# A four-layer graph network on one core: TensorE signals once per two units of nodes in layer 0 and once per quad in layer 3

## The chip, the cores and the metric

The kernel runs on one core of one Trainium2 chip. The metric is the device time of one execution in microseconds (us). The engines are TensorE (PE, with its weight loads shown apart as PEld), VectorE (DVE), ScalarE (ACT), GpSimd (POOL) and SyncE (SP), which only starts transfers here. Each engine works through its own queue of instructions in order. An engine that needs another's result waits on a semaphore, which the other one raises when a marked instruction is complete.

## The reference, cut to what matters

There are 8192 nodes with 32 features, and 262144 edges sorted by destination. Four layers run one after the other, each followed by a residual sum and a layer normalisation.

```python
x = ln(x + segment_sum(einsum('ei,eio->eo', x[src], weight[edge_type]), dst))   # layer 0, 64 types
x = ln(x + segment_sum(x[src] * edge_weight[:, None], dst))                     # layer 1
x = ln(x + segment_sum(x[src], dst))                                            # layer 2
h = relu(edge_feat @ W1 + b1)                                                   # layer 3
w = (h @ W2 + b2).reshape(e, 4, 8, 8)
m = products of s[src], v[src], edge_sh with w      # 8 scalars, 8 vectors of 3
x = ln(x + segment_sum(m, dst) + self_part(x))
```

## The kernel before

The change lies in `raw_layers`, in layers 0 and 3. A small class `Flow` holds an engine's queue: `mark(ins)` lets an instruction raise the engine's semaphore by one and returns the value that then stands for "done", and `after(mark)` makes the engine wait for such a value. A wait on a mark therefore covers all that the marking engine did before it.

**Gathers.** In both layers POOL fetches rows for 128 edges at a time, one indirect transfer each (`indirect`, L387), 2048 per layer. Layer 0 fetches rows of `fytab` (node features already multiplied with each type's weight), layer 3 rows of `fxtab`. POOL runs ahead of the other engines, but waits for a PE mark before it goes on: in layer 0 the rows of group g + 12 wait for marks of group g (L665, L671; the constant `AHEAD` is 12), in layer 3 those of quad q + 8 wait for the mark of quad q (`fetch_rows`, L842, called at L926; `AHEAD` is 8). Inside `gathers` it also waits for the transfers of two batches before, eight transfers to a batch.

**Layer 0** walks over 256 groups of 1024 edges. For group g, DVE makes a one-hot of the destinations (`one_hot`, L509), waits for the rows, and splits them into three bf16 parts (`parts`, L624 to L629). PE adds the parts up by destination (eight matmuls, L662) into a slot of bank 0 or 1 of the accumulator memory: four groups share a bank, and the two banks take turns. After four groups, `bank_out` (L635) reduces the bank to `win` with one DVE instruction. Every 32 groups `windows` (L499) and `normalize` (from L458) finish a chunk of 1024 nodes.

In the same loop, from group 8 on, `matrices` makes the dense matrices that layers 1 and 2 will use: 256 sets, nearly one per group, finished with group 251. For a set, DVE writes three one-hots (L562, L564, L567); PE turns them into four units of eight nodes (L576), each unit filling two of the banks 2 to 6 with 16 matmuls; PE marks each unit, and ACT copies its banks out in four instructions (L581, L582). SP then stores the set to `famat` and `fcmat` (L586, L587). `oh_free`, `bank_free` and `agg_free` hold the marks that allow a one-hot, a bank or an accumulator to be written again.

**Layers 1 and 2** load the stored matrices and multiply them (L761, L764). They begin when all of layer 0 is done.

**Layer 3** walks over 512 quads of 512 edges; two quads make one of the 256 groups, and eight quads a batch of edge data. One pass q of the loop issues on PE, in this order:

- H (`hidden(q + 2)`, L899, even q only): the first matrix of the edge network for two quads, then a mark on which ACT applies the relu (L907);
- w (L923): the second matrix for quad q into one of two pairs of banks, then a mark, on which DVE's products of quad q wait (L960, L963, L967);
- a (L932): the sums by destination of the older quad c = q - `LAG3`, with `LAG3` = 4, into bank 0 or 1 by the parity of its group, then a mark.

The waits of these: w(q) needs the relu of quad q and DVE's products of quad q - 2 to be done (the pair of banks is read). a(c) needs DVE's pass c + 2 and, for the first quad of a group, that DVE has read out the group two before (`agg_free`).

DVE's pass q does, in order: `factors` for the next two quads (L863 to L870, even q, waits for the gathered rows), small parts of quads q - 2 and q - 1 (L946, L951), the one-hot (L509), the products of quad q, and, when quad q - `LAG3` - 1 ends a group, the read-out of that group (L988, L989, L991), which waits for the mark of its a. `p` has six buffers; the one of quad q is free when a(q - 6) is marked. Every 32 groups `windows` and `normalize` finish a chunk here too.

Of the kernel before, what the change touches and what calls it, by code (L numbers as in the profile page):

```python
# [15 lines left out]
AF = mybir.ActivationFunctionType  # L16
OP = mybir.AluOpType
AX = mybir.AxisListType
# [3 lines left out]
P = 128  # L22
N = 8192
E = 262144
D = 32
R = 64
NB = N // P
# [7 lines left out]
GT = 8  # L35
GG = TT // GT
WS = N // GG
WT = 32
LC = 8
# [106 lines left out]
def raw_layers(tc, x, a, w0, w1, b1, w2, si, m, bad):  # L146
# [34 lines left out]
    def now(f):  # L181
        return (f.sem, f.n)
# [211 lines left out]
    n = 0  # L394
# [88 lines left out]
    def windows(c, acc, free):  # L483

        d0 = c * LC
        todo = []
        for j in [0, 1, 2, 3, -2, -1, 4]:
            lo, hi = 0, LC
            while 4 * (d0 + lo) + j < 0:
                lo += 1  # L490
            while 4 * (d0 + hi - 1) + j >= GG:
                hi -= 1
            if lo < hi:
                todo.append((j, lo, hi))
        wv = win.rearrange("p (d j) f -> p d j f", j=4)
        PE.after(*free)
        for n, (j, lo, hi) in enumerate(todo):
            g0 = 4 * (d0 + lo) + j
            ins = PE.e.matmul(acc[:, lo * D:hi * D].rearrange("p (d f) -> p d f", f=D),  # L499
                              shift[:, P - WS * j:2 * P - WS * j], wv[:, g0 // 4:g0 // 4 + hi - lo, g0 % 4, :],  # L500
                              start=(n == 0), stop=(n == len(todo) - 1))
        return PE.mark(ins)

    def ready(c):

        return min(GG, 4 * (LC * (c + 1) - 1) + 5)

    def one_hot(o, t, n):
        return V.e.tensor_tensor(o, iota[:, None, :].to_broadcast([P, n, P]),  # L509
                                 rel[:, t:t + n, None].to_broadcast([P, n, P]), op=OP.is_equal)  # L510
# [34 lines left out]

    acc_free = [None]
    oh_used = [None, None]
    bank_free = {k: (acc_free[0] if k == 2 else None) for k in range(2, 7)}
    st_ld = [Landing(tc, f"st_m{k}") for k in range(2)]
    w_up = [None]  # L550
    units = [0]

    def matrices(i):

        b, pp, k0 = i % 2, i // 2, 16 * (i % 2)
        WB = 8
        if i % WB == 0:
            n = min(WB * 16, CB * 16 - i * 16)
            V.after(now(V))
            own(V, V.e.tensor_copy(w_ps[:, 0:n], meta_w.rearrange("p n k -> p (n k)")[:, i * 16:i * 16 + n]))  # L560
        V.after(oh_used[b])
        own(V, V.e.tensor_tensor(oh_k[:, b, :, 0, :], iota[:, None, 0:64].to_broadcast([P, 16, 64]),  # L562
                                 meta_k[:, pp, k0:k0 + 16, None].to_broadcast([P, 16, 64]), op=OP.is_equal))
        V.e.tensor_tensor(oh_l[:, b], iota[:, None, :].to_broadcast([P, 16, P]),  # L564
                          meta_l[:, pp, k0:k0 + 16, None].to_broadcast([P, 16, P]), op=OP.is_equal)
        wo = (i % WB) * 16
        vm = V.mark(V.e.tensor_tensor(oh_k[:, b, :, 1, :], oh_k[:, b, :, 0, :],  # L567
                                      w_ps[:, wo:wo + 16, None].to_broadcast([P, 16, 64]), op=OP.mult))
        PE.after(vm)
        for q in range(4):  # L570
            bk = [2 + (2 * units[0] + h) % 5 for h in range(2)]
            PE.after(*(bank_free[b5] for b5 in bk))
            for j in range(4):
                for h in range(2):
                    hs_ = slice(64 * h, 64 * h + 64)
                    ins = PE.e.matmul(bank[:, bk[h], :].rearrange("p (c s j) -> p c s j", s=64, j=4)[:, :, :, j],  # L576
                                      oh_l[hs_, b, 4 * q + j, :], oh_k[hs_, b, 4 * q + j], start=True, stop=True)
            pm = PE.mark(ins)
            A.after(pm, st_ld[b].mark() if q == 0 and st_ld[b].n else None)
            for h in range(2):  # L580
                A.e.activation(st_c[:, b, q, h], bank[:, bk[h], 0:256], AF.Copy)  # L581
                bank_free[bk[h]] = am = A.mark(A.e.activation(st_a[:, b, q, h], bank[:, bk[h], 256:512], AF.Copy))  # L582
            units[0] += 1
        oh_used[b] = pm
        S.after(am)
        st_ld[b].add(S.e.dma_start(amat[:, 2048 * i:2048 * (i + 1)], st_a[:, b].rearrange("p u h c -> p (u h c)")))  # L586
        st_ld[b].add(S.e.dma_start(cmat[:, 2048 * i:2048 * (i + 1)], st_c[:, b].rearrange("p u h c -> p (u h c)")))  # L587


    NS = TT // WT  # L590
    NO = 4
    oh_free = [None] * NO
    agg_free = [freed[0], freed[0]]
    G.after(r0, *y_done)
    V.after(*y_done)
    PE.after(*freed)
    FIRST = 8
    made = 0
    done = 0
    per = 4  # L600
    AHEAD = 12
    landed = {}
    sums_of = {}
# [25 lines left out]
        prev_parts[0] = V.mark(V.e.tensor_tensor(part[2], tf(r), tf(x_ps), op=OP.subtract))  # L629
        return prev_parts[0]  # L630

    def bank_out(n):

        V.after(sums_of[per * n + per - 1])
        agg_free[n % 2] = vm = V.mark(V.e.tensor_reduce(  # L635
            win[:, per * n:per * (n + 1), :], bank[:, n % 2, 0:per * 3 * D].rearrange("p (g c f) -> p g f c", c=3, f=D),
            AX.X, OP.add))
        return vm

    prev_parts = [None]  # L640
    for g in range(AHEAD):
        for h in range(2):
            fetch_rows(g, h, None)
    for g in range(GG + 2):
        if g >= 2 and (g - 2) % per == per - 1:
            vm = bank_out((g - 2) // per)
            while done < NB // LC and ready(done) <= g - 1:
                acc = bank[:, (g - 2) // per % 2, 0:LC * D]
                agg_free[(g - 2) // per % 2] = vm = normalize(0, done, acc, windows(done, acc, (vm,)), x_a, x_b)
                done += 1  # L650
        if g >= GG:
            continue
        h, bk, c = g % NO, (g // per) % 2, g % per
        if g == FIRST // 2:
            V.after(slots(), x_in)
        V.after(oh_free[h])
        one_hot(oh[:, h], g * GT, GT)
        PE.after(parts(g))
        if c == 0:
            PE.after(agg_free[bk])  # L660
        for t in range(GT):
            ins = PE.e.matmul(bank[:, bk, 3 * c * D:3 * (c + 1) * D], oh[:, h, t, :],  # L662
                              xp[:, g % 4, t].rearrange("p c f -> p (c f)"), start=(t == 0), stop=(t == GT - 1))
        oh_free[h] = sums_of[g] = PE.mark(ins)
        fetch_rows(g + AHEAD, 0, sums_of[g])  # L665
        if g >= FIRST:
            upto = min(CB, (g - FIRST + 1) * CB // (GG - FIRST - 4))
            while made < upto:
                matrices(made)
                made += 1  # L670
        fetch_rows(g + AHEAD, 1, now(PE))  # L671
    stored = [ld.mark() for ld in st_ld]


# [124 lines left out]
    vm = cut(2, WT, 3, 8)  # L799
    MW = 344  # L800
    NP, NO = 6, 6
    LAG3 = 4
    p = cut(NP, 4, MW)
    pr = cut(2, 4, 64)
    red = cut(2, 4, 8)
# [86 lines left out]
    def hidden(q):  # L892

        s = q // 8
        k = s % 3
        PE.after(batch[s]["e"], quad.get(q - 1, {}).get("h", h_free))
        for h in range(2):
            r = q % 4 + h
            ins = PE.e.matmul(bank[64 * h:64 * h + 64, 2, :], w1_s[r * D:(r + 1) * D, :],  # L899
                              ef[r * D:(r + 1) * D, k, (q % 8) // 4, :], start=True, stop=True,  # L900
                              tile_position=(r * D, 64 * h))
        pm = PE.mark(ins)
        if q % 8 == 6:
            ef_free[k] = pm
        for h in range(2):
            A.after(pm, quad.get(q + h - 4, {}).get("w"))
            quad[q + h] = dict(h=A.mark(A.e.activation(hs[0:64, (q + h) % 4], bank[64 * h:64 * h + 64, 2, :], AF.Relu,  # L907
                                                       bias=b1_s[64 * h:64 * h + 64])))
# [2 lines left out]
        fetch_rows(q)  # L911
    factors(0)
    PE.after(c_in, *zf)
    hidden(0)
    for q in range(NQ + LAG3 + 2):

        if q % 2 == 0 and q + 2 < NQ:
            hidden(q + 2)
        if q < NQ:
            k, wp = w_bank()  # L920
            PE.after(quad[q]["h"], w_free[k])
            for t in range(4):
                ins = PE.e.matmul(wp[:, t, :], hs[0:65, q % 4, t * P:(t + 1) * P], w2_s[0:65], start=True, stop=True)  # L923
            quad[q]["w"] = PE.mark(ins)
            quad[q]["k"] = k, wp
            fetch_rows(q + AHEAD)  # L926
        c = q - LAG3
        if 0 <= c < NQ:
            g = c // 2
            PE.after(quad[c + 2]["v"], agg_free[g % 2] if c % 2 == 0 else None)  # L930
            for t in range(4):
                ins = PE.e.matmul(bank[:, g % 2, 0:MW], oh[:, c % NO, t, :], p[:, c % NP, t, :],  # L932
                                  start=(c % 2 == 0 and t == 0), stop=(c % 2 == 1 and t == 3))
            quad[c]["a"] = PE.mark(ins)

        prev = (V.sem, V.n)
        if q % 2 == 0 and q + 2 < NQ:
# [533 lines left out]
```

## Time and profile before

| What | Value |
|---|---|
| median of 5 runs | 6433.94 us (6429.66 to 6434.11) |
| the profiled execution: its own time | 6430.87 us |
| the profiled execution: its span | 6429.0 us |
| PE / PEld / DVE busy | 4776.1 / 3448.2 / 4364.1 us |
| ACT / POOL busy | 1755.0 / 3972.4 us |
| first gather of layer 0, last gather of layer 0 (start) | 225.3, 2805.3 us |
| first gather of layer 3, last gather of layer 3 (start) | 3812.9, 6383.2 us |

The profile takes one execution and shows when each engine worked. The share of busy time is an average over four layers with different limits, so the stages are read one by one. For a group of instructions the profile gives the count, the busy time, the mean length of one, and the idle time of the engine just before them with what ended that idle time. "issue" there is the time in which the engine waited for nothing that the profile shows. In the timeline each row has the start, the length, the engine and the line; several instructions in a row are merged, and the brackets hold the idle time before the row. Matmul ends are modelled and overlap the next matmul.

### The profile page before, as it was taken

The page shows a single profiled execution, that of the slowest core. Times are in us where ns is not written, and L with a number is a line of the kernel's source. Part 1 is how long each engine was busy: PE and PEld are TensorE (multiplying, and loading weights), DVE is VectorE, ACT ScalarE, POOL GpSimd, SP SyncE. Part 2 cuts the span into 40 slices and gives each one's busy share as a digit, 9 for nine tenths or more (in the row PEclk, how much of TensorE's full clock was granted, in tenths as well). Part 3 has the DMA queues.
Part 4 walks back from the last instruction along what each step waited for, and adds up shares of the span by engine and source line. Part 5 has one row for each costly group of instructions (what it writes and reads, how often), then busy time and mean ns, then how long its engine had stood idle before and what let it go on. Part 6 is the DMA issues. An engine that isn't in the chain of part 4 may idle for free.

```text
span 6429.0 us, 89476 instructions
## 1 busy us (share of the span) xinstructions
PE 4776.1 (74%) x34036; PEld 3448.2 (54%) x34036; DVE 4364.1 (68%) x9246; ACT 1755.0 (27%) x4886; POOL 3972.4 (62%) x4174
## 2 busy tenths in 40 slices
PE   7356666566666565644446879999999999999998
PEld 3145555565556555532223446666666666666665
DVE  4288878888888888830000028788888888888887
ACT  5345444454445454520000001111111111111111
POOL 2677777777777777730000027777777777777775
PEclk7578878887778888777777979999999999999999
DMA  9457766666666666779999961111111111111111
GB/s 349 162 138 183 181 178 173 181 181 181 172 180 183 178 185 167 190 263 431 432 431 412 398 240 28 28 28 29 28 28 29 28 28 28 29 28 29 28 29 21
DMA packets 290756, 999.51 MB, mean 155 GB/s; under 512 B 99021, under 2 KB 175886, under 8 KB 250638
## 3 DMA queue, kind: packets, MB, share of 16 engines
q1 hardware_dynamic: 155742, 916.89, 38.0%
q0 software_dynamic: 134144, 73.67, 11.6%
q8 instruction: 272, 4.46, 0.3%
q10 hardware_dynamic: 432, 3.15, 0.2%
q14 instruction: 166, 1.36, 0.1%
HBM read 521.39 MB, written 471.99 MB: 155 GB/s over the span
## 4 chain that ended last, share of the span: by engine, by line
DMA 27%; PE 24%; POOL 20%; DVE 19%; issue 8%; ACT 1%; POOLq 0%; SPq 0%; DVEq 0%; ACTq 0%
POOL f_arena L387 20%; DMA f_arena<-fytab,f_row 8%; PE bank L932 8%; DMA f_arena<-famat 8%; PE bank L923 6%; DMA f_arena<-fxtab,f_src 6%; DVE f_arena L564 4%; DMA f_arena<-fcmat 3%; PE bank L761 2%; PE bank L576 2%; DVE f_arena L562 2%; DVE f_arena L567 2%; PE bank L764 2%; DVE f_arena L509 2%; DMA fytab<-f_arena 1%
## 5 line engine op out<-in xcount | busy, mean ns | idle before, releaser
L387 POOL DMA_INDIRECT f_arena<-fxtab,f_src x2048 | 1947.4, 951 | 1630.5 <-PE bank L730 1006.7
L387 POOL DMA_INDIRECT f_arena<-fytab,f_row x2048 | 1957.0, 956 | 652.5 <-issue 555.3
L576 PE MATMUL bank<-f_arena 64*128 64x128 f32 x16384 | 1356.3, 333 | 757.0 <-DVE f_arena L567 751.3
L576 PEld LDWEIGHTS bank<-f_arena 64*128 64x128 f32 x16384 | 1280.7, 242 | 823.1 <-DVE f_arena L567 789.3
L932 PE MATMUL bank<-f_arena 128*128 128x344 f32 x4096 | 1306.7, 461 | 0.0
L581 ACT ACTIVATE f_arena<-bank 128x256 bf16<-128x256 f32 x2048 | 869.9, 426 | 1228.2 <-PE bank L576 1203.0
L923 PE MATMUL bank<-f_arena 65*128 65x256 f32 x4096 | 1021.7, 393 | 69.0 <-DVE f_arena L967 68.4
L923 PEld LDWEIGHTS bank<-f_arena 65*128 65x128 f32 x4096 | 770.2, 193 | 421.7 <-DVE f_arena L967 138.2
L932 PEld LDWEIGHTS bank<-f_arena 128*128 128x128 f32 x4096 | 796.7, 195 | 356.4 <-issue 27.1
L907 ACT ACTIVATE f_arena<-bank,f_arena 64x512 f32<-64x512 f32 x512 | 351.0, 686 | 2111.9 <-PE bank L899 2105.4
L582 ACT ACTIVATE f_arena<-bank 128x256 f32<-128x256 f32 x2048 | 884.4, 433 | 0.0
L509 DVE TENSOR_TENSOR f_arena<-bank,f_rel 128x512 f32<-128x512 f32 (+1 forms) x768 | 660.1, 860 | 55.7 <-ACT f_arena L541 44.4
L564 DVE TENSOR_TENSOR f_arena<-bank,f_arena 128x2048 f32<-128x2048 f32 x256 | 586.5, 2291 | 8.7
L967 DVE TENSOR_TENSOR f_arena<-bank,f_arena 128x256 f32<-128x256 f32 x1536 | 551.8, 416 | 0.0
L761 PE MATMUL bank<-f_arena,f_x_b 128*32 128x256 f32 x4096 | 292.7, 456 | 335.7 <-DMA f_arena<-famat 335.7
L458 DVE TENSOR_TENSOR f_lnf<-bank,f_x_b 128x256 f32<-128x256 f32 x8 | 3.4, 425 | 605.2 <-PE bank L741 605.2
L761 PEld LDWEIGHTS bank<-f_arena,f_x_b 128*32 128x32 f32 x4096 | 144.6, 131 | 472.5 <-DMA f_arena<-famat 311.0
L863 DVE TENSOR_TENSOR f_arena<-f_arena 128x192 f32<-128x192 f32 x256 | 93.6, 365 | 390.6 <-DMA f_arena<-fxtab,f_src 389.3
L963 DVE TENSOR_TENSOR f_arena<-bank,f_arena 128x512 f32<-128x512 f32 x512 | 349.1, 682 | 0.0
L662 PE MATMUL bank<-f_arena 128*128 128x96 bf16 x2048 | 140.7, 216 | 265.3 <-DVE f_arena L629 265.2
L624 DVE TENSOR_SCALAR bank<-f_arena 128x256 int32<-128x256 int32 x256 | 107.9, 422 | 306.8 <-DMA f_arena<-fytab,f_row 306.5
L562 DVE TENSOR_TENSOR f_arena<-bank,f_arena 128x1024 f32<-128x1024 f32 x256 | 312.0, 1219 | 1.1
(133 smaller groups left out, 3765.5 us busy)
## 6 DMA issues: line engine op xcount, KB each, us to landing
famat<-f_arena SPq DMA_DIRECT2D x256, 1024.0 KB
fcmat<-f_arena SPq DMA_DIRECT2D x256, 512.0 KB
fytab<-f_arena SPq DMA_DIRECT2D x64, 1024.0 KB, 11.5
f_arena<-fytab,f_row POOLq DMA_INDIRECT x2048
f_arena<-fxtab,f_src POOLq DMA_INDIRECT x2048
f_arena<-laid_ea SPq DMA_DIRECT2D x64, 512.0 KB, 3.6
f_arena<-laid_ea SPq DMA_DIRECT2D x64, 64.0 KB
f_arena<-laid_xT ACTq DMA_DIRECT2D x1, 1024.0 KB, 8.2
```

What stands on the lines that cost most here:

```text
L387: return G.e.indirect_dma_start(out=dest, out_offset=None, in_=table, in_offset=bass.IndirectOffsetOnAxis(ap=ix, axis=0))
L509: return V.e.tensor_tensor(o, iota[:, None, :].to_broadcast([P, n, P]), rel[:, t:t + n, None].to_broadcast([P, n, P]), op=OP.is_equal)
L562: own(V, V.e.tensor_tensor(oh_k[:, b, :, 0, :], iota[:, None, 0:64].to_broadcast([P, 16, 64]), meta_k[:, pp, k0:k0 + 16, None].to_broadcas ...
L564: V.e.tensor_tensor(oh_l[:, b], iota[:, None, :].to_broadcast([P, 16, P]), meta_l[:, pp, k0:k0 + 16, None].to_broadcast([P, 16, P]), op=OP ...
L576: ins = PE.e.matmul(bank[:, bk[h], :].rearrange("p (c s j) -> p c s j", s=64, j=4)[:, :, :, j], oh_l[hs_, b, 4 * q + j, :], oh_k[hs_, b, 4 ...
L581: A.e.activation(st_c[:, b, q, h], bank[:, bk[h], 0:256], AF.Copy)
L582: bank_free[bk[h]] = am = A.mark(A.e.activation(st_a[:, b, q, h], bank[:, bk[h], 256:512], AF.Copy))
L761: ins = PE.e.matmul(bank[q * D:(q + 1) * D, b, 0:256].rearrange("p (u h j) -> p u h j", h=2, j=4), x_b[:, s, :], mv[:, s], start=(s < 4), ...
L907: quad[q + h] = dict(h=A.mark(A.e.activation(hs[0:64, (q + h) % 4], bank[64 * h:64 * h + 64, 2, :], AF.Relu, bias=b1_s[64 * h:64 * h + 64])))
L923: ins = PE.e.matmul(wp[:, t, :], hs[0:65, q % 4, t * P:(t + 1) * P], w2_s[0:65], start=True, stop=True)
L932: ins = PE.e.matmul(bank[:, g % 2, 0:MW], oh[:, c % NO, t, :], p[:, c % NP, t, :], start=(c % 2 == 0 and t == 0), stop=(c % 2 == 1 and t = ...
L967: ins = V.e.tensor_tensor(pq[:, :, 128 + 64 * mm:192 + 64 * mm].rearrange("p t (o i) -> p t o i", i=8), wp[:, :, 192:256].rearrange("p t ( ...
```

## The change

In layer 0, `matrices` marks PE after every second unit only. The units take banks 1 to 6 in turn (three units in rotation), and ACT copies out two units after each mark. The sums of a group use one accumulator in bank 0: `sums_out` replaces `bank_out` and reduces each group by itself, one group later in DVE's order, behind `parts` of the next group. The group's own mark falls away: its sums count as done with the first mark of the set made in that group. POOL's two waits take the first and the last mark of the set.

In layer 3, one mark per pass stands behind w and covers H, a and w. `LAG3` becomes 5, and in a pass PE issues H(q + 2), then a(q - 5), then w(q). The relu is issued behind the pass's mark (`nonlinear`).

```diff
-    bank_free = {k: (acc_free[0] if k == 2 else None) for k in range(2, 7)}
+    bank_free = {k: None for k in range(1, 7)}
+    def banks_of(u):
+        return [1 + (2 * u + h) % 6 for h in range(2)]
...
+        marks = []
         for q in range(4):
-            bk = [2 + (2 * units[0] + h) % 5 for h in range(2)]
+            bk = banks_of(units[0])
+            units[0] += 1
             PE.after(*(bank_free[b5] for b5 in bk))
...
+            if q % 2 == 0:
+                continue
             pm = PE.mark(ins)
-            A.after(pm, st_ld[b].mark() if q == 0 and st_ld[b].n else None)
-            for h in range(2):
-                A.e.activation(st_c[:, b, q, h], bank[:, bk[h], 0:256], AF.Copy)
-                bank_free[bk[h]] = am = A.mark(A.e.activation(st_a[:, b, q, h], bank[:, bk[h], 256:512], AF.Copy))
-            units[0] += 1
+            marks.append(pm)
+            A.after(pm, st_ld[b].mark() if q == 1 and st_ld[b].n else None)
+            for u in range(2):
+                bk = banks_of(units[0] - 2 + u)
+                for h in range(2):
+                    A.e.activation(st_c[:, b, q - 1 + u, h], bank[:, bk[h], 0:256], AF.Copy)
+                    bank_free[bk[h]] = am = A.mark(A.e.activation(st_a[:, b, q - 1 + u, h], bank[:, bk[h], 256:512], AF.Copy))
...
-    def bank_out(n):
-        V.after(sums_of[per * n + per - 1])
-        agg_free[n % 2] = vm = V.mark(V.e.tensor_reduce(
-            win[:, per * n:per * (n + 1), :], bank[:, n % 2, 0:per * 3 * D].rearrange("p (g c f) -> p g f c", c=3, f=D),
-            AX.X, OP.add))
+    def sums_out(g):
+        V.after(sums_of[g])
+        return V.mark(V.e.tensor_reduce(win[:, g, :], bank[:, 0, 0:3 * D].rearrange("p (c f) -> p f c", f=D), AX.X, OP.add))
...
+            one_hot(oh[:, h], g * GT, GT)
+            PE.after(parts(g))
+        if g:
+            agg_free = sums_out(g - 1)
...
+        PE.after(agg_free)
         for t in range(GT):
-            ins = PE.e.matmul(bank[:, bk, 3 * c * D:3 * (c + 1) * D], oh[:, h, t, :],
...
+            ins = PE.e.matmul(bank[:, 0, 0:3 * D], oh[:, h, t, :], xp[:, g % 4, t].rearrange("p c f -> p (c f)"),
+                              start=(t == 0), stop=(t == GT - 1))
-        oh_free[h] = sums_of[g] = PE.mark(ins)
-        fetch_rows(g + AHEAD, 0, sums_of[g])
+        marks = []
...
-                matrices(made)
+                marks += matrices(made)
                 made += 1
-        fetch_rows(g + AHEAD, 1, now(PE))
+        if not marks:
+            marks.append(PE.mark(ins))
+        oh_free[h] = sums_of[g] = marks[0]
+        fetch_rows(g + AHEAD, 0, marks[0])
+        fetch_rows(g + AHEAD, 1, marks[-1])
...
-    LAG3 = 4
+    LAG3 = 5
...
-        pm = PE.mark(ins)
+        return ins
+
+    def nonlinear(q, pm):
...
         if q % 2 == 0 and q + 2 < NQ:
             hidden(q + 2)
-        if q < NQ:
...
-            quad[q]["w"] = PE.mark(ins)
-            fetch_rows(q + AHEAD)
         c = q - LAG3
         if 0 <= c < NQ:
...
-            quad[c]["a"] = PE.mark(ins)
+        if q < NQ:
+            k, wp = w_bank()
+            PE.after(quad[q]["h"], w_free[k])
+            for t in range(4):
+                ins = PE.e.matmul(wp[:, t, :], hs[0:65, q % 4, t * P:(t + 1) * P], w2_s[0:65], start=True, stop=True)
+            quad[q]["k"] = k, wp
+        if q < NQ + LAG3:
+            pm = PE.mark(ins)
+        if q < NQ:
+            quad[q]["w"] = pm
+            fetch_rows(q + AHEAD)
+        if 0 <= c < NQ:
+            quad[c]["a"] = pm
+        if q % 2 == 0 and q + 2 < NQ:
+            nonlinear(q + 2, pm)
```

More of the change, by code (lines that the diff above doesn't have):

```diff
@@ L587, in matrices @@
         st_ld[b].add(S.e.dma_start(cmat[:, 2048 * i:2048 * (i + 1)], st_c[:, b].rearrange("p u h c -> p (u h c)")))
+        return marks
     NS = TT // WT
@@ L592, in raw_layers @@
     oh_free = [None] * NO
-    agg_free = [freed[0], freed[0]]
+    agg_free = freed[0]
     G.after(r0, *y_done)
@@ L599, in raw_layers @@
     done = 0
-    per = 4
     AHEAD = 12
@@ L630, in parts @@
         return prev_parts[0]
-    def bank_out(n):
-        V.after(sums_of[per * n + per - 1])
-        agg_free[n % 2] = vm = V.mark(V.e.tensor_reduce(
-            win[:, per * n:per * (n + 1), :], bank[:, n % 2, 0:per * 3 * D].rearrange("p (g c f) -> p g f c", c=3, f=D),
-            AX.X, OP.add))
-        return vm
+    def sums_out(g):
+        V.after(sums_of[g])
+        return V.mark(V.e.tensor_reduce(win[:, g, :], bank[:, 0, 0:3 * D].rearrange("p (c f) -> p f c", f=D), AX.X, OP.add))
     prev_parts = [None]
@@ L643, in raw_layers @@
             fetch_rows(g, h, None)
[L644 to L649, printed above, removed]
-                done += 1
[L651 to L660, printed above, removed]
+    for g in range(GG + 1):
+        h = g % NO
+        if g < GG:
+            if g == FIRST // 2:
+                V.after(slots(), x_in)
+            V.after(oh_free[h])
+            one_hot(oh[:, h], g * GT, GT)
+            PE.after(parts(g))
+        if g:
+            agg_free = sums_out(g - 1)
+            while done < NB // LC and ready(done) <= g:
+                acc = bank[:, 0, 256:256 + LC * D]
+                agg_free = normalize(0, done, acc, windows(done, acc, (agg_free,)), x_a, x_b)
+                done += 1
+        if g == GG:
+            break
+        PE.after(agg_free)
         for t in range(GT):
-            ins = PE.e.matmul(bank[:, bk, 3 * c * D:3 * (c + 1) * D], oh[:, h, t, :],
-                              xp[:, g % 4, t].rearrange("p c f -> p (c f)"), start=(t == 0), stop=(t == GT - 1))
-        oh_free[h] = sums_of[g] = PE.mark(ins)
-        fetch_rows(g + AHEAD, 0, sums_of[g])
+            ins = PE.e.matmul(bank[:, 0, 0:3 * D], oh[:, h, t, :], xp[:, g % 4, t].rearrange("p c f -> p (c f)"),
+                              start=(t == 0), stop=(t == GT - 1))
+        marks = []
         if g >= FIRST:
@@ L901, in hidden @@
                               tile_position=(r * D, 64 * h))
-        pm = PE.mark(ins)
+        return ins
+    def nonlinear(q, pm):
         if q % 8 == 6:
-            ef_free[k] = pm
+            ef_free[(q // 8) % 3] = pm
         for h in range(2):
@@ L913, in raw_layers @@
     PE.after(c_in, *zf)
-    hidden(0)
+    nonlinear(0, PE.mark(hidden(0)))
     for q in range(NQ + LAG3 + 2):
@@ L918, in raw_layers @@
             hidden(q + 2)
-        if q < NQ:
[L920 to L923, printed above, removed]
-            quad[q]["w"] = PE.mark(ins)
-            quad[q]["k"] = k, wp
-            fetch_rows(q + AHEAD)
         c = q - LAG3
```

## The prediction

> **What bounds the kernel now.** I read the costliest groups first, then the view of the line that leads them, then the waits, then timelines of a few groups. POOL's gathers are the two costliest groups:
>
> ```profile
> L387 POOL DMA_INDIRECT f_arena<-fxtab,f_src x2048 | 1947.4, 951 | 1630.5 <-PE bank L730 1006.7
> L387 POOL DMA_INDIRECT f_arena<-fytab,f_row x2048 | 1957.0, 956 | 652.5 <-issue 555.3
> ```
>
> One gather takes 0.95 us, and the idle time before it, without the single 1006.7 us of layers 1 and 2, is (1630.5 - 1006.7) / 2047 = 0.305 us each, nearly all put down to "issue": POOL waits for nobody. The view of this line gives the first and last start:
>
> ```profile
> L387 POOL DMA_INDIRECT f_arena<-fytab,f_row x2048: 939/944/8351, 225.3 to 2805.3; - x187
> L387 POOL DMA_INDIRECT f_arena<-fxtab,f_src x2048: 940/944/1127, 3812.9 to 6383.2; - x187
> ```
>
> So layer 0 takes 2580.0 / 2047 = 1.260 us per gather (four early ones took 5.75 to 8.35 us) and layer 3 takes 2570.3 / 2047 = 1.2556 us. The span is 225.3 + 2580.0 + 1007.6 (layers 1 and 2 with their seams) + 2570.3 + 45.8 = 6429.0 us. 5150 us of it are POOL's issue alone. The waits say the same from the other side, DVE is held up by rows that are not there yet:
>
> ```profile
> DVE f_arena L863 <- DMA f_arena<-fxtab,f_src: 389.3, 181, 8.9
> DVE bank L624 <- DMA f_arena<-fytab,f_row: 306.5, 107, 10.5
> ```
>
> The chain of waits names PE at 24%, but that is a chain through waits whose other arm is equally late; a faster PE would only wait for rows. The change touches neither the gathers nor their number. It can act in three places: if it makes POOL wait, in the seam after layer 0 (2805.3 us to the first load of layer 1 at 2819.78), and in the last 45.8 us.
>
> **Layer 0, part by part.** A group has eight gathers, 8 x 1.2483 = 9.99 us (30 gathers from 230.29 to 267.74 us give the undisturbed pitch 1.2483). What DVE and PE need for a group is seen here:
>
> ```profile
> 1501.11 6.69 PE L576 MATMUL bank<-f_arena 64*128 64x128 f32 x64 [4.52 <-DVE f_arena L567]
> 1503.07 0.43 DVE L624 TENSOR_SCALAR bank<-f_arena 128x256 int32<-128x256 int32 x1 [0.89 <-DMA f_arena<-fytab,f_row]
> 1504.94 0.38 ACT L581 ACTIVATE f_arena<-bank 128x256 bf16<-128x256 f32 x1 [0.50 <-PE bank L576]
> 1508.91 1.21 DVE L567 TENSOR_TENSOR f_arena<-f_arena,bank 128x1024 f32<-128x1024 f32 x1
> 1511.64 0.42 DVE L624 TENSOR_SCALAR bank<-f_arena 128x256 int32<-128x256 int32 x1
> ```
>
> DVE's cycle without a wait is 1511.64 - 1503.07 = 8.57 us, with one four-group reduce in it (L635, 0.55 us, start to next start 0.47). The single-group reduce that replaces it is not in the trace. By L988 (128 elements, 280 ns) and L989 (192, 348 ns) 96 elements cost about 246 ns; bounds are 0.17 us (L460, eight elements) and 0.28 us. I take 0.25. In busy time that adds 256 x 0.25 - 35.2 = 29 us to DVE, which the 306.5 us of waiting for rows cover.
>
> The new wait in front of it is for the first mark of the set before, that is for 32 matmuls after L567. Here L567 ended at 1501.05, and the second unit was there by 1504.94, after 3.9 us; in the next but one group 64 matmuls take 4.28 us, so 32 take about 2.2. DVE comes there after one-hot and parts, 1514.09 - 1510.12 - 0.47 = 3.5 us after L567. The wait is 0 to 0.4 us; behind it stand the three one-hots and PE's sums. I take 0.2. Cycle: 8.57 - 0.47 + 0.25 + 0.2 = 8.55 us, at most 8.75, against 9.99. Every 32 groups a chunk is finished as before, and DVE makes that up at over 1 us per group.
>
> PE's sums now wait for the reduce of the group before, 0.25 us, while DVE writes one-hots for 4.7 us anyway: nothing. A fourth unit waits for the first to be copied out (four ACT instructions, 1.07 us, as long as a unit of 64 matmuls in 4.28): a few tenths, before the next set 8 us later. ACT ends a set, and SP issues its two stores, about one unit later; the last set is stored some 30 us before layer 1 loads. POOL's marks come up to 8 us later (behind the one-hots and a pair), but DVE's waits for rows show that POOL is only one or two groups ahead, and it stops at twelve: about 100 us spare. Layer 0: 0.
>
> Seam: the last parts end at 2810.05, sums take 0.82, the reduce 0.56. Now the reduce of group 254 (0.25) stands ahead of the sums and 0.25 replaces 0.56: within -0.3 and +0.3, I take 0.
>
> **Layer 3.** PE issues the same matmuls; H moves in front of an a. The weight loads of PE show its pace where it waits for nothing, just after a chunk was finished:
>
> ```profile
> 4196.81 1.71 PEld L923 LDWEIGHTS bank<-f_arena 65*128 65x128 f32 x8
> ...
> 4201.17 0.19 PEld L899 LDWEIGHTS bank<-f_arena 32*64 32x64 f32 x4 [0.48 <-issue]
> ...
> 4203.80 2.15 PEld L932 LDWEIGHTS bank<-f_arena 128*128 128x128 f32 x8
> 4206.05 1.77 PEld L923 LDWEIGHTS bank<-f_arena 65*128 65x128 f32 x8
> ...
> 4210.47 0.19 PEld L899 LDWEIGHTS bank<-f_arena 32*64 32x64 f32 x4 [0.48 <-issue]
> ```
>
> H to H is 9.30 us for two quads; POOL takes 8 x 1.2556 = 10.04. PE's 96% busy between first and last gather (2461.6 of 2570.3 us, from the table by stage) is therefore not the bound, but its spare is only 0.74 us per pair. The marks left out number 756 in layer 0 (1280 to 524) and 762 in layer 3 (1280 to 518). Their price isn't shown alone: from 0 to the gaps beside them, 0.10 us after an a (2.15 from 4203.80 ends at 4205.95) and the 0.81 us of "issue" after H, which the change of tile shape may as well cause. I take 0; whatever it is, PE waits longer for it.
>
> [...]
>
> A relu now starts 4.1 us later (behind a and w), is 1.40 us, and has until w(q + 2), past a, w, H, a (7.4 us): covered. p and `w` marks: DVE had to wait for the mark of w in the pass before anyway, so a(q - 6) is covered by it. A new constraint: the first a of a group waits for the read-out two groups before, which moves one DVE pass later. Where PE is late, it has H, a, w (5.1 us) to do before that a, while DVE's products and read-out need 2.06 + 0.87 = 2.9 us: nothing. Where DVE is late, PE stalls some 2 us, but then rows set the pace. If that cover goes, PE is late next, then POOL.
>
> POOL's spare is least behind a chunk: the w at 4196.81 is quad 71 (group 32 is read out in pass 70), and POOL waits for it before gather 316, due at 3812.9 + 316 x 1.2556 = 4209.7; that is 10.8 us. The chunk now comes a DVE pass later (3.8 us), with one w less behind it (1.8): w(72) is 2 us later, about 9 us stay. Layer 3's pace: 0.
>
> **The last 45.8 us** move. PE works without a gap there:
>
> ```profile
> 6385.46 0.36 DVE L863 TENSOR_TENSOR f_arena<-f_arena 128x192 f32<-128x192 f32 x1 [1.88 <-DMA f_arena<-fxtab,f_src]
> ...
> 6392.52 1.08 DVE L967 TENSOR_TENSOR f_arena<-bank,f_arena 128x256 f32<-128x256 f32 x3
> 6392.57 2.15 PEld L932 LDWEIGHTS bank<-f_arena 128*128 128x128 f32 x8
> ...
> 6396.62 11.44 PEld L932 LDWEIGHTS bank<-f_arena 128*128 128x128 f32 x40
> ...
> 6408.74 0.29 DVE L988 TENSOR_REDUCE f_arena<-bank 128x8 f32<-128x128 f32 x1 [3.87 <-PE bank L932]
> ```
>
> The a at 6392.57 is quad 506, the first of its group. It will wait for a read-out that follows the products ending at 6393.6, 0.8 earlier since the pass before loses its own: 6392.8 + 0.7 + 0.1 = 6393.6, so 1.0 us late. The a of quad 508 would start 1.0 + 2.29 behind 6396.62, at 6399.9, and waits for the read-out after pass 511 (ends 6400.57 now, about 6400.1 then): 6400.9, another 1.0. Three more follow without a wait. Together +2.0; bounds 0 and +4.6 (two whole steps of 2.29).
>
> Sum against the profiled execution: 6430.87 + 0 + 0 + 0 + 2.0 = 6432.9 us. That execution lies 3.1 below the median of the runs, so the forecast for the median is 6433.94 + 2.0 = 6435.9.
>
> **Rivals.** (1) *PE's marks were dear and PE sets layer 3's pace.* For it: PE's 96% and its share in the chain. Against: no wait of POOL. POOL's undisturbed pitch allows 2047 x 1.2483 = 2555.3, so the gain ends at 15.0 us: 6421. (2) *Slower: the first a of each group waits in layer 3 and PE becomes the bound.* It decides once the exposed wait passes PE's spare of 0.74 us per pair; a wait of 1.3 us, say, would give (1.3 - 0.74) x 256 - 9 = +134, 6568. For it: PE's spare is small and it slows after idling (8 a's matmuls, 2.48 us at 5005.02, took 4.79 at 5018.01 after a stall). Against: the 2.2 us of cover above. (3) *Slower: DVE waits for the set's first mark in layer 0.* It decides at 9.99 - 8.55 = 1.4 us more per group; 1 us beyond that costs 244 - 100 = +144, 6578. That marks do not become fewer is ruled out by the code.
>
> [...]
>
> **The numbers.** Forecast 0.90, (1) 0.02, (2) 0.05, (3) 0.03. A measurement of this kernel can tell about 0.2%, 12.9 us, from no change: faster 0.02, same 0.90, slower 0.08. The forecast's own range is 6430 (runs 4 below the median, no tail cost) to 6441 (tail 4.6); smaller mishaps of the kind of (2), a few us of POOL waiting behind some of the eight chunks, widen it to 6426 to 6448.
>
> **What would show it.** Right: gathers of layer 0 still take 2580 us and of layer 3 2570 us from first to last, with 0.30 us before each; DVE waits less for rows in layer 0; the stretch after the last gather is 48 us. Wrong: POOL waits on L576 or L923 well over 0.3 us each, or DVE on PE at the new reduce by over a us.

## The result, and the profile after

The changed kernel takes 6438.19 us (median of 24 runs, 6433.35 to 6443.08) and the kernel before 6433.99 us (44 runs, 6429.66 to 6441.93): a ratio of 1.0005 with a 95% interval of 1.0000 to 1.0011. That is 4.2 us more, within 0.2%, where 2.0 more were forecast. The profiled execution has a span of 6433.6 us, 4.6 more than before. Some of the experiments below ran on chips on which the kernel before takes 7510 or 7594 us, and each is compared within its own set of runs only.

The two groups of gathers on the page of the changed kernel, and their first and last start in the view of that line:

```profile
L387 POOL DMA_INDIRECT f_arena<-fxtab,f_src x2048 | 1949.5, 952 | 1631.5 <-PE bank L739 1007.7
L387 POOL DMA_INDIRECT f_arena<-fytab,f_row x2048 | 1957.5, 956 | 652.5 <-issue 568.4
```

```profile
L387 POOL DMA_INDIRECT f_arena<-fytab,f_row x2048: 940/944/11274, 224.6 to 2804.9; - x187
L387 POOL DMA_INDIRECT f_arena<-fxtab,f_src x2048: 940/944/1146, 3813.5 to 6385.9; - x187
```

POOL's idle time per gather in layer 3 is (1631.5 - 1007.7) / 2047 = 0.305 us, the same as before: it still waits for nobody. The span splits into 224.6 + 2580.3 + 1008.6 + 2572.4 + 47.7 us, against 225.3 + 2580.0 + 1007.6 + 2570.3 + 45.8. So layer 0's gathers cost 0.3 us, the middle 1.0, layer 3's gathers 2.1, and the end 1.9. DVE still waits for rows, somewhat less than before in both layers (the view of the waits, with the total, the number of times and the longest, in us):

```profile
DVE f_arena L872 <- DMA f_arena<-fxtab,f_src: 335.6, 176, 8.7
DVE bank L633 <- DMA f_arena<-fytab,f_row: 290.6, 95, 10.5
```

The same view has the two new waits, of PE for the moved read-out in layer 3 and of DVE for a set's first mark in layer 0:

```profile
PE bank L936 <- DVE f_arena L1009: 69.8, 65, 1.8
DVE f_arena L644 <- PE bank L581: 15.3, 46, 0.4
```

The end was forecast row by row. In the timeline of the last 50 us, PE's weight loads and DVE's read-outs of the changed kernel:

```profile
6396.26 0.18 DVE L1009 TENSOR_TENSOR f_arena<-bank,f_arena 128x24 f32<-128x24 f32 x1
...
6396.49 2.04 PEld L936 LDWEIGHTS bank<-f_arena 128*128 128x128 f32 x8 [0.36 <-DVE f_arena L1009]
...
6403.36 0.18 DVE L1009 TENSOR_TENSOR f_arena<-bank,f_arena 128x24 f32<-128x24 f32 x1
...
6403.66 9.00 PEld L936 LDWEIGHTS bank<-f_arena 128*128 128x128 f32 x32 [1.08 <-DVE f_arena L1009]
```

Both waits stand where they were expected, each behind the read-out of the group two before: the first a of group 253, and the first a of group 254 with the three a's behind it. Before, the last five a's ran without a gap. The two waits are 0.36 + 1.08 = 1.44 us. Besides, PE itself came later to the first of them: counted from the last gather, the a before it began 0.9 us later than in the kernel before (6392.11 - 6385.89 against 6388.52 - 6383.16 us).

What the marks cost is seen in a stretch of layer 3 where PE waits for nobody, behind the first chunk, in the timeline of the weight loads:

```profile
4201.41 0.19 PEld L908 LDWEIGHTS bank<-f_arena 32*64 32x64 f32 x4 [0.33 <-issue]
4202.42 2.04 PEld L936 LDWEIGHTS bank<-f_arena 128*128 128x128 f32 x8 [0.81 <-issue]
...
4206.36 2.15 PEld L936 LDWEIGHTS bank<-f_arena 128*128 128x128 f32 x8
4208.61 1.77 PEld L942 LDWEIGHTS bank<-f_arena 65*128 65x128 f32 x8
4210.71 0.19 PEld L908 LDWEIGHTS bank<-f_arena 32*64 32x64 f32 x4 [0.33 <-issue]
```

H to H is 4210.71 - 4201.41 = 9.30 us, as before. The a at 4206.36 ends its loads at 4208.51 and w follows 0.10 us later; the gap of 0.10 us stood there before too, when a was marked. The 0.81 us behind H stayed too. Neither gap was the mark's.

### The profile page after: what moved, and what is told of

Its sections match the earlier page's. It is cut to its first block, busy times and chain, and to the rows that moved or that the text cites. A ratio compares the mean times of both kernels' runs of the same rounds, so it can differ in the third digit from the quotient of the medians.

```text
span 6433.6 us, 89897 instructions
## 1 busy us (share of the span) xinstructions
PE 4805.0 (75%) x34036; PEld 3451.4 (54%) x34036; DVE 4389.5 (68%) x9438; ACT 1753.7 (27%) x4886; POOL 3975.0 (62%) x4174
## 4 chain that ended last, share of the span: by engine, by line
DMA 26%; POOL 25%; PE 23%; DVE 15%; issue 10%; ACT 1%; POOLq 0%; SPq 0%; DVEq 0%; ACTq 0%
POOL f_arena L387 25%; DMA f_arena<-famat 8%; PE bank L936 7%; DMA f_arena<-fytab,f_row 7%; DMA f_arena<-fxtab,f_src 6%; PE bank L942 5%; DVE f_arena L567 3%; DMA f_arena<-fcmat 3%; PE bank L581 3%; PE bank L770 2%; PE bank L773 2%; DVE f_arena L565 2%; DVE f_arena L570 2%; DMA fytab<-f_arena 2%; PE bank L908 1%
## 5 line engine op out<-in xcount | busy, mean ns | idle before, releaser
L387 POOL DMA_INDIRECT f_arena<-fxtab,f_src x2048 | 1949.5, 952 | 1631.5 <-PE bank L739 1007.7
L581 PE MATMUL bank<-f_arena 64*128 64x128 f32 x16384 | 1383.2, 337 | 792.0 <-DVE f_arena L570 707.5
L581 PEld LDWEIGHTS bank<-f_arena 64*128 64x128 f32 x16384 | 1303.6, 246 | 861.9 <-DVE f_arena L570 744.8
L936 PE MATMUL bank<-f_arena 128*128 128x344 f32 x4096 | 1333.4, 468 | 70.1 <-DVE f_arena L1009 69.8
L591 ACT ACTIVATE f_arena<-bank 128x256 bf16<-128x256 f32 x2048 | 834.5, 407 | 1231.3 <-PE bank L581 1211.2
L936 PEld LDWEIGHTS bank<-f_arena 128*128 128x128 f32 x4096 | 763.3, 193 | 637.9 <-issue 224.9
L942 PE MATMUL bank<-f_arena 65*128 65x256 f32 x4096 | 978.8, 381 | 9.4 <-DVE f_arena L985 9.2
L942 PEld LDWEIGHTS bank<-f_arena 65*128 65x128 f32 x4096 | 778.4, 190 | 208.1 <-DVE f_arena L985 21.4
L592 ACT ACTIVATE f_arena<-bank 128x256 f32<-128x256 f32 x2048 | 849.9, 415 | 0.0
L570 DVE TENSOR_TENSOR f_arena<-f_arena,bank 128x1024 f32<-128x1024 f32 x256 | 309.7, 1210 | 0.0
```

The lines of the kernel that those rows point to most:

```text
L387: return G.e.indirect_dma_start(out=dest, out_offset=None, in_=table, in_offset=bass.IndirectOffsetOnAxis(ap=ix, axis=0))
L591: A.e.activation(st_c[:, b, q - 1 + u, h], bank[:, bk[h], 0:256], AF.Copy)
L592: bank_free[bk[h]] = am = A.mark(A.e.activation(st_a[:, b, q - 1 + u, h], bank[:, bk[h], 256:512], AF.Copy))
```

## The experiments

The runs fell on three chips. The kernel before took 6448.03 us beside the four kernels of the first table, 7510.02 us beside `l0_only`, `l3_only`, `readout_back` and `lag4`, and 7593.84 us beside `half_chunk_late`, `l0_again`, `l3_again` and `chunk_late`. Ratios are against the kernel before in the same set.

**POOL's pace taken away.** In four kernels every second gather of layers 0 and 3 is left out, so that what its pace hides is seen. The rest of the work is the same, on rows that were never fetched.

```diff
-            indirect(xg[:, k, t, :], table[:, :], ix[:, s * WT + t:s * WT + t + 1]).then_inc(ld.sem, 16)
-            ld.n += 16
+            if t % 2 == 0:
+                indirect(xg[:, k, t, :], table[:, :], ix[:, s * WT + t:s * WT + t + 1]).then_inc(ld.sem, 16)
+                ld.n += 16
```

The kernel before with this edit:

> The kernel before, with only every second gather issued in layers 0 and 3 (the rows of the other tiles are never fetched, so the sums are made from what lies in the buffer): POOL needs 2 x 1024 x 1.25 us and sets no pace any more. DVE (8.5 us per group) should pace layer 0 and PE (9.30 us per pair of quads) layer 3. Where the kernel before takes 6434 us, this should take some 350 to 420 us less: 2580 becomes about 2290 between POOL's start and the end of layer 0, 2570 becomes about 2450 in layer 3.

The changed kernel with it:

> The changed kernel with only every second gather issued, as in half_before, so that what POOL's pace hides is seen. Theory A (marks are free; the new waits are short): layer 0 is 25 to 80 us slower than in half_before (0.11 us of more reduce and up to 0.2 us of waiting for the set's first mark, per group), layer 3 equal within 20 us, since H to H stays at 9.30 us where PE is late. [...] Theory B (PE's new wait for the read-out costs pace where nothing hides it): layer 3 is over 50 us slower.

The changed kernel with it, and with the old marks put back:

```diff
             if q % 2 == 0:
+                PE.mark(ins)
                 continue
...
+        if g >= FIRST and g < GG - 4:
+            PE.mark(ins)
...
-            hidden(q + 2)
+            PE.mark(hidden(q + 2))
...
+            if q < NQ:
+                PE.mark(ins)
```

> half_after with every mark of the kernel before put back (behind each unit, the sums, H and a), with nobody waiting for the added ones. Theory A: as half_after within 5 us, H to H unchanged. [...]

The changed kernel with it, and with the read-out moved:

```diff
-        c = q - LAG3 - 1
+        c = q - LAG3
         if 0 <= c < NQ and c % 2 == 1:
```

> half_after with the read-out of layer 3 moved back into the pass that adds up the group's last quad. Theory A: layer 3 within 20 us of half_after. Theory B: the waits of a for the read-out go, and layer 3 gets faster by most of what half_after lost against half_before.

Medians of four runs each; the stages are those of the profiled executions, from POOL's first gather to the first load of layer 1, and from POOL's first gather in layer 3 to the end:

| Kernel | median us | layer 0 | layer 3 |
|---|---|---|---|
| half_before | 5970.06 | 2283.9 | 2448.3 |
| half_after | 6024.24 | 2311.4 | 2475.8 |
| half_marks | 6024.51 | 2320.3 | 2479.9 |
| half_readout_back | 6028.92 | 2317.8 | 2476.0 |

With half the gathers the kernel before is 478 us faster than in full, so the gathers do set the pace. That is more than the 350 to 420 us expected, although both stages came within 7 us of theirs: the expected 2450 us of layer 3 run to the end, and the 2570 us that they were held against stop at the last gather. The change now costs 54 us, about half of it in each layer; the full kernel hides that under POOL. `half_marks` takes the same time as `half_after` (0.3 us more; the four runs of each spread over 19 and 24 us), and in all four kernels H to H is 9.30 us in 244 of 255 pairs, with five marks in a pair or with two. So some 1500 marks more or less are worth nothing that these runs can see. In layer 0 the 27.5 us were within what was expected. DVE's busy time in that stage grew by 21.7 us (2125.3 to 2147.0), of which the reduces alone are 29.6 (35.2 to 64.8). The other 5.9 us are idle time, mainly this: DVE waits 20.8 us for the set's first mark (71 waits in `half_after`), but 16.6 us less for the matmuls of the chunks (51.3 to 34.7).

Layer 3 went neither as theory A nor as theory B had it. It lost 27.5 us, and moving the read-out back gave nothing. The long pairs are those in which one of the seven chunks before the last is finished: 13.0 to 13.1 us in `half_before`, 15.4 to 18.4 in `half_after`. Added up over the seven they make 26.1 of the 27.5 us. The timeline of PE shows the second of them, in `half_before` and in `half_after` (L500 here is the `windows` matmul):

```profile
4158.19 1.99 PE L924 MATMUL bank<-f_arena 65*128 65x256 f32 x8
4160.02 2.48 PE L933 MATMUL bank<-f_arena 128*128 128x344 f32 x8
4163.06 3.26 PE L500 MATMUL bank<-f_arena,f_shift 128*128 128x256 f32 x14 [0.56 <-DVE f_arena L992]
```

```profile
4199.81 1.89 PE L943 MATMUL bank<-f_arena 65*128 65x256 f32 x8
4204.57 4.76 PE L500 MATMUL bank<-f_arena,f_shift 128*128 128x256 f32 x14 [2.88 <-DVE f_arena L1010]
```

Before, an a of 2.48 us stood between w and the chunk, and DVE made its products of that w and the read-out meanwhile. In the new order w is the last of the pass: PE idles 2.88 us through the products and the read-out, and behind this idle time the chunk's matmuls also run slower (4.76 against 3.26 us; in the six chunks between 4000 and 5800 us 26.6 against 19.6 us). The granted clock fell to 0.50 there from 4204.2 to 4207.6 us. It fell so at four of the seven chunks of `half_after`, and at none of these seven in `half_before`, where PE idles 0.56 us.

**That cause alone.** The chunk is finished one group later, on a read-out that is long done:

```diff
-            agg_free[g % 2] = gm
-            while done < NB // LC and ready(done) <= g + 1:
+            last, old, agg_free[g % 2] = g == GG - 1, agg_free[1 - g % 2], gm
+            while done < NB // LC and ready(done) <= (g + 1 if last else g):
...
-                w_free[k] = normalize(3, done, acc, windows(done, acc, (w_free[k], gm)), z, x_a)
+                w_free[k] = normalize(3, done, acc, windows(done, acc, (w_free[k], gm if last else old)), z, x_a)
```

> half_after (only every second gather issued, the other rows never fetched), with each chunk of layer 3 finished one group later, on the read-out of the group before, which is long done; the last chunk as before. In half_after H to H is 9.30 us in 244 of 255 pairs and layer 3 is 27 us slower than in half_before; I put that down to the eight pairs with a chunk (15.4 to 18.4 us against 13.1), where PE has nothing queued between w and the chunk and idles through DVE's products and read-out. If so, layer 3 falls by 20 to 30 us against half_after, to 2445 to 2455 us from the first gather to the end. If the loss is in the read-out waits or the order of H, a and w, it stays near 2476.

Layer 3 takes 2448.2 us, as `half_before` (2448.3); the pairs with a chunk fell to 12.3 us. So the loss of layer 3, where PE sets the pace, lies in the chunks and goes with this idle time. (That the two totals agree so closely is partly chance: the chunks here are 0.8 us shorter than in `half_before`, and one early pair is 5 us longer.) The median, 6025.38 us, shows none of that: this run was on another chip, and its layer 0 took 2342.1 us there, with 186.1 us of "issue" idle before PE's L582, which `half_after` does not have.

**Parts of the change by themselves**, made by joining layers 0 to 2 of one kernel and layer 3 of the other:

> Only the layer 0 part of the change; layer 3 as before. Theory A (POOL's gathers set the pace of both layers, marks are free, the whole cost is PE's wait for the moved read-out in the last 48 us): same time as before, within 1 us; from the first to the last gather of layer 0 still about 2580 us. Theory B (the new waits inside the loops leak into POOL's pace): 1 to 2 us more, since layer 0's part then carries a part of the measured 4 us.

> Only the layer 3 part of the change; layer 0 as before. Theory A: all of the loss, 2 to 4 us over before, with 47.7 us from the last gather to the end where before has 45.8. Theory B: the same stretch after the last gather, but also over 2 us more between the first and last gather of layer 3 than the 2570.3 of before.

> The whole change, but DVE reads a finished group out in the pass in which PE adds up its last quad (it has waited for that pass's mark anyway), not one pass later. Theory A: PE's waits for the read-out (69.8 us in 65 places with the change) nearly vanish, the stretch after the last gather falls from 47.7 to about 45.8 us, and the time falls by 2 us against the whole change. Theory B: the pace of layer 3 falls too, back to 2570 us from first to last gather, so 4 us in all.

> The whole change with LAG3 left at 4, so a(q-4) stands before w(q). Theory A: gathers keep their pace, since a cycle from DVE's products through a, w and the next products is about 6.5 us for two quads against 10.04 of POOL; one a less follows the last w, so the last stretch is about 45.2 us and the time 2 to 3 us below the whole change. Rival: w now stands behind an a that waits for DVE, DVE waits for w in every pass, and layer 3 slows by over 0.1 us per quad, 50 us or more.

The set fell on a chip where the kernel before takes 7510.02 us, and there another limit holds. In `l3_only`, whose layer 0 is that of the kernel before, the waits of POOL read:

```profile
POOL f_arena L387 <- PE bank L662: 448.2, 192, 20.6
POOL f_arena L387 <- remote: 343.0, 140, 5.3
POOL f_arena L387 <- PE bank L933: 179.3, 58, 7.8
POOL f_arena L387 <- PE bank L576: 136.0, 28, 9.8
```

POOL now stands still for PE's marks. ("remote" is a wait whose end the profile can't put down to an instruction.) A gather still takes 0.944 us and DVE is busy for 4374.3 us, against 4364.1 in the profile of the kernel before; PE has idle "issue" time inside its runs of matmuls, 294.2 us before L662 and 162.4 before L576, where the profile of the kernel before shows none. With PE as the bound both parts of the change cost: `l0_only` 1.0035 (1.0023 to 1.0048), `l3_only` 1.0046 (1.0033 to 1.0059), and both with the read-out moved, `readout_back`, 1.0073 (1.0060 to 1.0087). `lag4` gives 1.0079 (1.0066 to 1.0092). The whole change as it stands was not run in this set. The stretch after the last gather is 58.0 us with layer 3 of before (`l0_only`), 65.9 in `l3_only`, 65.4 in `readout_back` and 58.9 in `lag4`. That looks as if the longer end went with `LAG3` = 5, but the set below contradicts it: `l0_again`, whose layer 3 is that of before, has 64.2 us and `l3_again` 64.1. These ends, of one profiled execution each, tell nothing about the change. `readout_back` did not do what was expected of it, and `lag4` can't be told apart from it. As a test of the 2 to 4 us, the set is inconclusive. It was repeated in part:

> The layer 0 part alone once more, beside before on a chip where before takes 6430 to 6450 us. Theory A: within 1.5 us of before. Theory B: 2 us or more above it.

> The layer 3 part alone once more, beside before on a chip where before takes 6430 to 6450 us. Theory A: 2 to 4 us above before, 47.7 us after the last gather. If the 4 us of the whole change come half from layer 0, this is only about 2 us above.

> The same edit in the whole changed kernel, with all gathers. Theory A: nothing to gain, POOL's pace covers the eight stalls: within 2 us of the change, the stretch after the last gather 47.7 us. Where PE is slow enough to be waited for, 20 us less than the change.

This set met the same limit: `l0_again` 1.0053 (1.0039 to 1.0067), `l3_again` 1.0031 (1.0019 to 1.0044), both beside 7593.84 us. `chunk_late`, the whole change with the late chunks, is at 1.0039 (1.0026 to 1.0051), less than the two parts together (1.0084); its interval overlaps those of both parts. The whole change itself was not run in this set either, so the 20 us expected there are not measured. No version tried beats the kernel before.

## Why the prediction was right

**What bounds the kernel.** Right. First to last gather is 2580.3 and 2572.4 us with the same 0.305 us between gathers, and half the gathers take away 478 us.

**Layer 0.** Right at 0: 0.3 us between first and last gather. The single-group reduce takes 0.252 us (0.25 taken), the wait for the first mark is 15.3 us in 46 places, 0.4 us at most, as bounded. The units wait for ACT by 83.2 us in all (171 waits, 0.5 us on average and 2.0 at most), the "few tenths" of the prediction. Without POOL's cover these things cost 27.5 us.

**The price of the marks.** Right at 0: with POOL's cover gone, putting the marks back left the time as it was (6024.51 against 6024.24 us, in runs that spread over 19 and 24 us).

**Layer 3's pace.** The time is right, one reason was incomplete. The wait for the moved read-out came to 69.8 us in 65 places at L936, at most 1.8 us, and cost nothing where rows set the pace; in `half_after`, where PE is late, it was 0.6 us in all, as argued. What the working missed is that the chunk's matmuls lost the a that stood between them and w. It moved the chunk by "a DVE pass later" with "one w less behind it" and made that 2 us of POOL's spare; the size is 26.1 / 7 = 3.7 us per chunk, and the mechanism is PE's idle 2.88 us in front of the chunk, with slower matmuls in four of seven. The 9 us of spare cover it: in the full kernel POOL's waits on L942 are 18.6 us in 61 places, 0.3 us each, no more than before any gather.

The forecast also has no term for a PE that runs slower behind stalls of some 2 us, though a row given for rival (2) spoke for one: the 4.79 us at 5018.01 come just after a stall of 2.64 us. In the changed kernel one of the new waits reads

```profile
4176.95 4.26 PE L936 MATMUL bank<-f_arena 128*128 128x344 f32 x8 [1.83 <-DVE f_arena L1009]
```

where eight such matmuls otherwise take 2.48 us; the granted clock is 0.50 from 4177.0 to 4180.4 us. So behind a stall of 1.83 us these matmuls took another 1.78 us. This too was covered by POOL's pace here.

**The end.** 45.8 became 47.7 us, +1.9 for a forecast of +2.0, with both waits that were named. That the size agrees so well is partly luck: the first wait was 0.36 us and not 1.0, and the rest came from PE, which reached it 0.9 us later by itself; the prediction had no such term. Its upper bound of 6441 us comes out only if the end's 4.6 us are added to the forecast, which already holds 2.0 of them; from 6433.94 it is 6438.5, and the result lies just inside.

**The other 2 to 3 us.** The seam and the layers between (+1.0) and layer 3's gathers (+2.1) were forecast at 0. The 2.1 us are not waits: POOL's busy time on these gathers went from 1947.4 to 1949.5 us with the idle time the same. They lie in gathers that overlap a `factors` instruction of DVE: counted in the traces, these are 14.5 us longer in all than 944 ns each before, and 16.1 us after; the others are not longer. The prediction took a gather's length as fixed. On the other two chips POOL's busy time on layer 3's gathers is also higher with the changed layer 3: 1943.4 us in `l3_only` against 1939.3 in `l0_only`, and 1943.2 in `l3_again` against 1938.7 in `l0_again`. That points to the change in layer 3, but with half the gathers `half_after` shows no such growth over `half_before`, and one execution of each kernel does not prove it. The 1.0 us stays open.

**The rivals.** (1) is refuted by `half_marks`, within the spread of its runs. (2) and (3) did not come about: both waits exist, but neither reached POOL where POOL sets the pace. On the chips where POOL waits for PE, each part of the change loses 0.3 to 0.5%; by which of the waits was not separated there.

## What to carry to other kernels

Find the engine that never waits, count its instructions, and see how long the others could be late before it notices; a change that only touched those others moved the end here, by 1.9 us, and little else (2.1 us of that engine's own instructions, which got longer). Fewer marks were no gain in themselves: some 1500 of them put back changed the time by 0.3 us, far inside the spread of the runs (`half_marks`), while a mark that came later made its reader later: DVE waited 20.8 us for the set's first mark in `half_after`. When an instruction is moved in an engine's queue, look at what it covered: the a between w and the chunk hid DVE's products, and nobody waited for it.

## What the runs showed of the hardware

The same kernel before took 6448, 7510 and 7594 us on three chips. On the two slower ones POOL's gathers of layer 3 had their usual length (1938.7 to 1943.4 us for all 2048, against 1947.4), and DVE was busy for about its usual time in `l3_only` (4374.3 against 4364.1 us). But PE had idle "issue" time within its runs of matmuls (162.4 us before L576 in `l3_only`, 548.8 before the same line, there L581, in `chunk_late`), and waits of ACT, DVE and POOL ended without a visible cause (ACT waited 1418.4 us in 95 places for "remote" in `l3_only`, 1380.4 us in 96 in `chunk_late`). With half of the gathers left out, the chip of the 7594 us gave 6025.38 us (`half_chunk_late`) and the one of the 6448 us 6024.24 us (`half_after`). So nearly all of the slowness goes when half of the gathers go, in one kernel on one of these chips. Whether it is their number, or that half of the rows are then never fetched, and by what way, no run here shows.

PE's granted clock differed too: on average 0.85 in the runs of the kernel before at 6448 us, 0.77 to 0.79 in those at 7510 and 7594, and 0.87 to 0.89 with half of the gathers on either chip. In layer 0 it was 0.68 in `l3_only` against 0.80 in the kernel before (300 to 2400 us of each). As many stalls of PE come with the lower clock in these traces (below), this can be a consequence of PE's idle time as well as a cause of more; the runs don't separate them.

The granted clock in the traces is either 1.0 or 0.5 and changes in steps of 3.41 us: in the profiles of the kernels before and after, each of the 492 and 502 stretches at one clock, but for the first and the last, is a multiple of 3.413 us long. It fell around stalls of PE that were shorter than such a step, the 1.83 us above for one, and not at each: of the 26 waits of over 1.5 us before L936 in the changed kernel, 13 came with the half clock and 13 did not, and of the seven stalls of 2.88 us in `half_after`, four did and three did not.

Gathers that overlap DVE's `factors` (L863 to L870 before the change) lasted on average 51 to 57 ns longer than the usual 944 ns, counted in the trace; all other lines of DVE's quad work stay under 5 ns. These gathers, some 250 to 280 for each of the five instructions, make up all of the 14 us by which layer 3's gathers are longer than 2048 undisturbed ones. In the changed kernel it is 58 to 63 ns and 16 us.
